# Expert layers as seven block products instead of eight, with the sums on VectorE and GpSimd

## The chip, the cores and the metric

The kernel runs on one core of one Trainium2 chip. The metric is the device time of one execution in microseconds. Three runs of the kernel before took 1371.4, 1369.11 and 1367.32 us; the median is 1369.11.

The profile names the engines so: PE is the TensorE matmul, PEld its weight loads, DVE is VectorE, ACT is ScalarE, POOL is GpSimd and SP is SyncE. SP, ACT and POOL also issue DMA transfers.

## What is computed

The whole program is a mixture of experts, a linear attention, a conditioned attention and two layers of local attention with a feed-forward network, over 4 x 512 tokens of width 256, all in float32. The change is in the mixture of experts alone:

```python
TOP_K = 2                                     # E = 8 experts, H = 256, M = 512
gate_w = jax.nn.softmax(gate, axis=-1)
topk_w, topk_i = jax.lax.top_k(gate_w, TOP_K)
cw = jnp.sum(jax.nn.one_hot(topk_i, E) * topk_w[..., None], axis=-2)
h1 = jax.nn.relu(jnp.einsum('bsh,ehm->bsem', x, W1) + b1)
h2 = jax.nn.relu(jnp.einsum('bsem,emn->bsen', h1, W2) + b2)
out_e = jnp.einsum('bsen,enh->bseh', h2, W3) + b3
return jnp.einsum('bseh,bse->bsh', out_e, cw)
```

Only the two experts chosen for a token matter, so the kernel sorts the 2 x 2048 pairs of token and expert by expert and computes only those.

## The kernel before

**Slots.** The sorted pairs are laid into slots of one expert each. `SLOTS` lists 24: 15 of 256 rows (two tiles of 128, `d.n == 2`) and nine of 128 rows. Their order is 1, 2, 2 twice, then 1, 2, 2, 2 three times, then 1, 2, 2, then 1, where 1 stands for a slot of 128 rows and 2 for one of 256; two more of 128 rows stand behind a branch and run only if they are needed. The 22 that always run are the list `often`. `rowtok` says which token each row of a slot takes, and `goal` to which row of the DRAM buffer `ys` its result goes. A row of padding has the entry 0 in both maps: it gathers token 0 and writes row 0 of `ys`.

**One slot.** `loads` brings the expert's weights in three transfers on SP: `w1` (with the biases of both layers in its first eight columns), `w2` and `w3`, two buffers each. A buffer's next load waits until everything that read the buffer's last contents is done. `gather` fetches the slot's rows of x with one indirect DMA per tile, issued by POOL, transposes them on PE, and copies them to SBUF as `xbT`. `layer` is used twice: h1 from `xbT` with `w1` (two chunks of the contraction), and h2 from h1 with `w2` (four chunks). In a slot of 256 rows a layer has four output blocks of 128 units, each a chain of 128x128 weights against 256 tokens, two blocks to a PSUM bank; `relu` adds the bias and takes the maximum with zero, alternately on ACT and DVE. `last` is the third layer: tokens as the stationary side, `w3` moving, then an addition of the bias on DVE into `ob`, and one indirect DMA per tile that scatters `ob` to `ys`, issued by POOL. A scatter waits until the scatter before it has landed, since both write `ys`.

**Order.** In the loop over `often` (from line 1506), iteration j writes down: layer one of slot j, `last` of slot j-1, loads and gather of slot j+1, one of the `later` weight loads, layer two of slot j. The framework's scheduler may move instructions within this, by priority and its own estimate of time, except those given to `keep_in_program_order`. PE's instructions are kept so only where `PE.in_order()` is set; in the loop that is the transposes of a gather.

**PSUM.** `banks("ps0", mm=4, tp=2, acc=2)` gives four banks to the layers, two to transposes and two to the third layer.

**Afterwards.** `results` reads `ys` back by token, and `weighted` makes the weighted sum into the four tiles `y[b]`, which stand unused until then.

Of the kernel before, what the change touches and what calls it, by code (L numbers as in the profile page):

```python
# [12 lines left out]
F32 = mybir.dt.float32  # L13
I32 = mybir.dt.int32
AF = mybir.ActivationFunctionType
# [5 lines left out]
NT = S // 128  # L21
# [21 lines left out]
NRARE = 2  # L43
NROWT = 2 * NPAIR + NHALF
NHI = 2 * NROWT
MCONST = (128, 128 + NE, 2 * NE, 2, NE * NE, NHI, 2 * B * NT, 64, NE)
NMC = sum(MCONST)


# [18 lines left out]
def adaln_attn_ffn_kernel(ctx: ExitStack, tc: tile.TileContext, a: dict, out: bass.AP):  # L68
# [1093 lines left out]
    with ExitStack() as abc:  # L1162
# [5 lines left out]


        with ExitStack() as moe:  # L1170
            moe.enter_context(banks("ps0", mm=4, tp=2, acc=2))
            xp = moe.enter_context(tc.tile_pool(name="xp", bufs=1, reuse_waits="tile"))
            ew = moe.enter_context(tc.tile_pool(name="ew", bufs=2, reuse_waits="tile"))
            hp = moe.enter_context(tc.tile_pool(name="hp", bufs=2, reuse_waits="tile"))
# [13 lines left out]
            for n in MCONST:  # L1188
                parts.append(mc[:, at : at + n])
                at += n  # L1190
            mtri, mtiles, mthr, mslot, mlow, miota, mtok, mfold, mwt = parts


            ys = dr.tile([1 + 2 * B * S, H], F32, tag="ys", name="ys")
            xall = a["x"].rearrange("b s h -> (b s) h")


# [201 lines left out]
            pmap2 = acct("pmap2")  # L1399
            for q in range(2):  # L1400
                PE.matmul(pmap2[64 * q : 64 * q + 64, :NROWT], mfold, half_map[:, :, q], start=True, stop=True)
            goal = xp.tile([128, NROWT], I32, tag="goal", name="goal")
            nc.vector.tensor_copy(goal, pmap2[:, :NROWT])
            rowtok = xp.tile([128, NROWT], I32, tag="rowtok", name="rowtok")
            nc.vector.tensor_scalar(rowtok, pmap2[:, :NROWT], -1.0, 0.0, ALU.add, ALU.max)
            nc.vector.tensor_single_scalar(rowtok, rowtok, B * S - 1, op=ALU.bitwise_and)


            def busy(n):
# [7 lines left out]

            def relu(dst, src, bias):
                if turn[0]:
                    nc.scalar.activation(dst, src, AF.Relu, bias=bias)  # L1420
                else:
                    nc.vector.tensor_scalar(dst, src, bias, 0.0, ALU.add, ALU.max)  # L1422


            def place(kind, i):
# [11 lines left out]
                d.w3 = ew.tile([128, 5, H], F32, tag="w3", name="w3")  # L1437
                nc.sync.dma_start(d.w3, we[:, 8 + 6 * ME :].rearrange("p (c m) -> p c m", m=H))

            def gather(j, d):  # L1440
                xb = hp.tile([128, 2, H], F32, tag="xb", name="xb", bufs=3)
                for i in range(d.n):
                    r = place(d.n, SLOTS[j][0]) + i
                    nc.gpsimd.indirect_dma_start(
                        out=xb[:, i, :], out_offset=None, in_=xall,
                        in_offset=bass.IndirectOffsetOnAxis(ap=rowtok[:, r : r + 1], axis=0))
                n = d.n * 128
                pt = tpt("pxb")
                with PE.in_order():
                    for c in range(2):  # L1450
                        for i in range(d.n):
                            PE.transpose(pt[:, c * n + i * 128 : c * n + (i + 1) * 128],
                                         xb[:, i, c * 128 : (c + 1) * 128], ident)
                xbT = hp.tile([128, 2, 256], F32, tag="xbT", name="xbT")
                evac(xbT[:, :, 0:n], pt[:, : 2 * n].rearrange("p (c t) -> p c t", t=n))
                d.xbT = xbT

            def layer(d, src, tag, w, bias):
                n = d.n * 128
# [14 lines left out]
                        relu(dst[:, m, 0:n], ps[:, i * n : (i + 1) * n], d.w1[:, bias + m : bias + m + 1])  # L1474
                return dst

            def last(j, d):
                ps = acct("po")
                for i in range(d.n):
                    mm(ps[:, i * H : (i + 1) * H],  # L1480
                       [(d.h2[:, c, i * 128 : (i + 1) * 128], d.w3[:, c, :]) for c in range(4)])
                ob = hp.tile([128, 2, H], F32, tag="ob", name="ob", bufs=3)
                nc.vector.tensor_tensor(
                    ob[:, 0 : d.n, :], ps[:, : d.n * H].rearrange("p (i h) -> p i h", h=H),
                    d.w3[:, 4, :].unsqueeze(1).to_broadcast([128, d.n, H]), ALU.add)
                for i in range(d.n):
                    r = place(d.n, SLOTS[j][0]) + i
                    nc.gpsimd.indirect_dma_start(
                        out=ys, out_offset=bass.IndirectOffsetOnAxis(ap=goal[:, r : r + 1], axis=0),
                        in_=ob[:, i, :], in_offset=None)  # L1490


            later = {
# [5 lines left out]
            cond_weights(wp, lambda name, load: later.update({name: load}))  # L1499
            cw_ = {}  # L1500

            ds = [SimpleNamespace() for _ in SLOTS]
            loads(0, ds[0])
            gather(0, ds[0])
            often, rare = ds[:-NRARE], range(len(ds) - NRARE, len(ds))
            for j, d in enumerate(often):
                if j == len(often) - 1:
                    aside = conditions(cw_, wp)
                    next(aside)
                if j == len(often) - 2:  # L1510
                    halves = nc.values_load(nhalf[0:1, 0:1], min_val=0, max_val=2 * NE)
                if j == 1:
                    weights()
                h1 = layer(d, d.xbT, "h1", d.w1[:, 8:].rearrange("p (c m) -> p c m", m=ME), 0)
                if j:
                    last(j - 1, ds[j - 1])
                if j + 1 < len(often):
                    loads(j + 1, ds[j + 1])
                    gather(j + 1, ds[j + 1])
                    if j > 1 and later:  # L1520
                        name, behind[0] = next(iter(later)), True
                        cw_[name] = later.pop(name)()
                        behind[0] = False
                d.h2 = layer(d, h1, "h2", d.w2, 4)
            last(len(often) - 1, often[-1])

            next(aside)
# [1 line left out]
            with tc.If(halves > NHALF - NRARE):  # L1529
                for j in rare:  # L1530
                    d = ds[j]
                    loads(j, d)
                    gather(j, d)
                    h1 = layer(d, d.xbT, "h1", d.w1[:, 8:].rearrange("p (c m) -> p c m", m=ME), 0)
                    d.h2 = layer(d, h1, "h2", d.w2, 4)
                    last(j, d)
# [213 lines left out]
def _shape_constants():  # L1750
    f = np.float32
    p = np.arange(128)
    bmask = np.repeat((p[:, None] // 32 == p[None, :] // 32).astype(f)[:, None, :], 4, axis=1)
    hmask = np.where(p[:, None] // CHD == np.arange(8)[None, :], CHD**-0.5, 0.0)
    hmask = np.concatenate([hmask, p[:, None] // CHD % 2 == np.arange(2)[None, :]], axis=1).astype(f)
    i, j = p[:, None], p[None, :]
    lmask = np.concatenate([np.where(j >= i, 0.0, MASKED), np.where(j <= i, 0.0, MASKED)], axis=1).astype(f)

    kmask = np.concatenate([(j >= i % 64)[:, :64], (j <= i % 64)[:, :64], j >= i], axis=1).astype(f)

    e = np.arange(NE)
    thr = np.concatenate([256 * e + 128, 256 * e])
    slot = np.full((128, 2), -1)
    slot[: len(SLOTS), 0] = [i if n == 2 else NPAIR + i // 2 for i, n in SLOTS]
    slot[: len(SLOTS), 1] = [-1 if n == 2 else i for i, n in SLOTS]
    tile, expert = p // NE, p % NE
    mconst = np.concatenate(
        [(p[:, None] < p[None, :]).astype(f),
         ((tile[:, None] < tile[None, :]) & (expert[:, None] == expert[None, :])).astype(f),
         (expert[:, None] == e[None, :]).astype(f), np.tile(thr, (128, 1)).astype(f), slot.astype(f),  # L1770
         np.tile((e[None, :] <= e[:, None]).reshape(-1), (128, 1)).astype(f), np.tile(np.arange(NHI), (128, 1)).astype(f),
         (np.arange(2 * B * NT)[None, :] * 128 + p[:, None] + 1).astype(f),
         (p[:, None] % 64 == np.arange(64)[None, :]).astype(f),
         np.tile(np.where(e == NE - 1, 1 - NE, 1), (128, 1)).astype(f)], axis=1)

    pos = np.arange(S, dtype=f)
    inv = f(10000.0) ** np.repeat(np.arange(0, H, 2, dtype=f) / f(H), 2)
    peT = np.ascontiguousarray(np.sin(pos[:, None] / inv[None, :]).astype(f).T)

    half = np.arange(0, DHD, 2, dtype=f)  # L1780
    freqs = pos[:, None] * (f(1.0) / f(10000.0) ** (half / f(DHD)))[None, :]
    base = (half + f(0.4 * DHD)) / f(1.4 * DHD)
    scale = base[None, :] ** ((pos - f(S // 2)) / f(WIN // 2))[:, None]
    cos, sin = np.cos(freqs).astype(f), np.sin(freqs).astype(f)
    parts = []
    for sc in (f(8.0) * scale, f(1.0) / scale):
        c, s = cos * sc, sin * sc
        parts += [np.concatenate([c, c], 1), np.concatenate([-s, s], 1)]
    rot = np.stack(parts).astype(f).reshape(4, NT, 128, DHD).transpose(2, 0, 1, 3)
    return {"mconst": mconst, "bmask": bmask, "hmask": hmask, "lmask": lmask, "kmask": kmask, "peT": peT, "rot": rot}  # L1790
# [81 lines left out]
```

## Time and profile before

| what | us |
|---|---|
| median of three runs | 1369.11 |
| the profiled execution | 1364.1 |
| its span, first to last instruction | 1362.3 |
| PE busy (span share 96%) | 1302.8 |
| DVE busy (47%) | 645.4 |
| ACT busy (41%) | 563.9 |
| POOL busy (17%) | 227.1 |
| expert stage, 42 to 315 us: PE busy in it | 270.7 |
| the same stage: DVE, ACT, POOL busy | 58.5, 43.5, 77.4 |

A line of the profile's groups reads: source line, engine, operation, tile written and tiles read, shape, count; then the busy time of the group, the mean duration of one in ns, and the idle time of that engine just before, with what ended it. `ph` is the PSUM bank of the first two layers, `po` that of the third, `pxb` that of the transposes. Matmuls overlap in the array, so one record is longer (379 ns for 256 columns) than the distance to the next. A float32 matmul has two MATMUL records and two weight loads. Lines of a timeline or a chain begin with the start in us from the span's start and the length of the merged piece. A line of windows gives, for each stretch, busy time and count of PE, PEld, DVE, ACT and POOL, then PE's clock, the share of DMA busy and GB/s. Sources and tiles give the minimum, median and maximum duration in ns.

### The profile page before, as it was taken

The numbers are of one execution on the slowest core, as the hardware profiler recorded it, in microseconds if no ns is written. First come the engines' busy times: TensorE is split into PE (matmuls) and PEld (weight loads), VectorE is DVE, ScalarE is ACT, GpSimd is POOL, SyncE is SP. The second block draws the span as 40 slices with busy tenths as digits, with TensorE's granted clock in tenths as the row PEclk, the third lists the DMA queues.
The fourth block names the chain that finished last, engine by engine and source line by source line (L and its number), as shares of the span: only waits on it lengthen the run. The fifth ranks groups of instructions, "written<-read, shape, count | busy, mean of one in ns | idle before, by whom it ended". The sixth has DMA issues, their size and how long they took to land.

```text
span 1362.3 us, 25766 instructions
## 1 busy us (share of the span) xinstructions
PE 1302.8 (96%) x10700; PEld 850.1 (62%) x10700; DVE 645.4 (47%) x1343; ACT 563.9 (41%) x1111; POOL 227.1 (17%) x223
## 2 busy tenths in 40 slices
PE   5899999998999999999999999999999998999998
PEld 4788888884666644444435665766555566667654
DVE  6222212125777743332226777764362767765421
ACT  4111111125555456565655646552223565463111
POOL 1324322211000020010103322100030312210010
PEclk7999999999999999999999999999999999999999
DMA  4577666644000000000201011211001011011000
GB/s 135 205 244 280 228 231 240 211 155 136 1 1 1 0 1 1 1 0 1 90 5 67 13 29 37 81 42 25 24 1 43 24 34 26 19 42 50 20 20 26
DMA packets 43110, 95.02 MB, mean 70 GB/s; under 512 B 9568, under 2 KB 25192, under 8 KB 40168
## 3 DMA queue, kind: packets, MB, share of 16 engines
q1 hardware_dynamic: 37560, 81.81, 18.1%
q0 software_dynamic: 3792, 10.24, 2.2%
q8 instruction: 88, 1.44, 0.4%
q10 hardware_dynamic: 1632, 1.21, 0.3%
q14 instruction: 38, 0.31, 0.1%
HBM read 83.95 MB, written 7.21 MB: 67 GB/s over the span
## 4 chain that ended last, share of the span: by engine, by line
PE 83%; DVE 7%; ACT 6%; issue 2%; DMA 1%; POOL 0%; POOLq 0%; SPq 0%; DVEq 0%; ACTq 0%
PE ph L82 14%; PE pdq L82 10%; PE sc L82 6%; PE pfy L82 6%; PE pug L82 5%; PE pua L82 5%; PE pv L82 5%; PE po L82 5%; PE pdy L82 4%; PE pn L82 3%; PE pz L82 2%; PE pds L82 2%; ACT p L685 2%; PE pqk L82 1%; PE pur L82 1%
## 5 line engine op out<-in xcount | busy, mean ns | idle before, releaser
L82 PE MATMUL pdq<-wqkv,yT 128*128 128x512 f32 x384 | 171.2, 596 | 6.0 <-ACT yT L613 4.1
L425 ACT ACTIVATE cex<-sc 128x512 f32<-128x512 f32 x256 | 131.8, 607 | 84.5 <-PE sc L82 84.4
L82 PE MATMUL ph<-h,w 128*128 128x256 f32 (+1 forms) x704 | 132.8, 346 | 1.6 <-DVE h L1422 1.6
L639 POOL TENSOR_TENSOR qr<-t,t 128x512 f32<-128x512 f32 x64 | 81.3, 1271 | 297.4 <-DVE t L636 282.8
L82 PEld LDWEIGHTS pdq<-wqkv,yT 128*128 128x128 f32 x384 | 71.4, 190 | 90.3 <-issue 76.9
L82 PEld LDWEIGHTS ph<-h,w 128*128 128x128 f32 x704 | 116.1, 191 | 13.7 <-DVE h L1422 1.9
L1420 ACT ACTIVATE h<-ph,w 128x256 f32<-128x256 f32 (+1 forms) x88 | 35.3, 437 | 190.9 <-PE ph L82 130.5
L1422 DVE TENSOR_SCALAR h<-ph,w 128x256 f32<-128x256 f32 (+1 forms) x88 | 36.1, 438 | 161.1 <-PE ph L82 102.6
L685 ACT ACTIVATE p<-pds,ss 128x192 f32<-128x192 f32 (+1 forms) x256 | 82.3, 434 | 12.5 <-PE pds L82 11.2
L82 PE MATMUL sc<-qm,kT 32*128 32x512 f32 x512 | 86.8, 639 | 0.0
L629 ACT ACTIVATE sq<-pdq 128x512 f32<-128x512 f32 x64 | 38.4, 601 | 97.1 <-POOL qr L639 50.2
L82 PE MATMUL pug<-hT,w 128*128 128x512 f32 x160 | 75.9, 597 | 0.0
L82 PE MATMUL pua<-hT,w 128*128 128x512 f32 x160 | 75.2, 592 | 0.0
L82 PE MATMUL ph<-xbT,w 128*128 128x256 f32 (+1 forms) x352 | 68.7, 347 | 0.5 <-ACT xbT L127 0.5
L82 PE MATMUL po<-w,h 128*128 128x256 f32 x296 | 67.6, 379 | 0.0
L395 POOL TENSOR_SCALAR fterm<-vw,faT 128x256 f32<-128x256 f32 x16 | 14.6, 922 | 312.1 <-DVE cr L385 259.6
L789 ACT ACTIVATE gl<-pug,cols 128x512 f32<-128x512 f32 x40 | 27.3, 687 | 86.5 <-PE pug L82 86.4
L82 PEld LDWEIGHTS ph<-xbT,w 128*128 128x128 f32 x352 | 58.5, 191 | 7.2 <-ACT xbT L127 0.7
L82 PE MATMUL pfy<-w,uA 128*128 128x256 f32 x256 | 61.2, 382 | 0.0
L82 PEld LDWEIGHTS pn<-p,v 64*64 64x64 f32 x1792 | 44.1, 136 | 27.4 <-issue 10.1
L82 PE MATMUL pv<-cex,v 128*32 128x512 f32 x512 | 61.2, 597 | 0.0
L82 PEld LDWEIGHTS po<-w,h 128*128 128x128 f32 x296 | 55.7, 190 | 8.1 <-ACT h L1420 0.9
(304 smaller groups left out, 2182.7 us busy)
## 6 DMA issues: line engine op xcount, KB each, us to landing
w<-in_moe_w_dram SPq DMA_DIRECT2D x22, 1024.0 KB
w<-in_moe_w_dram SPq DMA_DIRECT2D x22, 640.0 KB
w<-in_moe_w_dram SPq DMA_DIRECT2D x22, 516.0 KB
zb<-rows SPq DMA_DIRECT2D x32, 256.0 KB
g<-ys SPq DMA_DIRECT2D x6, 512.0 KB
wqkv<-in_f_wqkv_dram SPq DMA_DIRECT2D x2, 1536.0 KB
w<-in_f_w_dram SPq DMA_DIRECT2D x2, 1408.0 KB
out_dram<-yc SPq DMA_DIRECT2D x16, 128.0 KB
```

What stands on the lines that cost most here:

```text
L82: cls._queue(nc.tensor.matmul(*args, **kw))
L395: nc.gpsimd.tensor_scalar_mul(fterm[:, t, :], vw, W["faT"][:, t, b : b + 1])
L425: nc.scalar.activation(ex[:, i, :], pss[2 * j + i], AF.Exp, scale=CHD**-0.5)
L629: nc.scalar.activation(sq, p3, AF.Square)
L639: nc.gpsimd.tensor_tensor(qr_t[:, s], t1, t2, ALU.add)
L685: nc.scalar.activation(p[:, at : at + n], pss[j // 2][r][:, at % 384 : at % 384 + n], AF.Exp, scale=d.ss[:, j, 1, 2 * c + r : 2 * c + r + 1])
L789: nc.scalar.activation(gl, pg, AF.Gelu, bias=col("bg", l * (NU + 1) + i))
L1420: nc.scalar.activation(dst, src, AF.Relu, bias=bias)
L1422: nc.vector.tensor_scalar(dst, src, bias, 0.0, ALU.add, ALU.max)
```

## The change

A layer of a 256-row slot is seen as a product of 2x2 blocks: the weights halved along inputs and along outputs, the tokens halved along inputs and into two tiles of 128. Eight block products make it plainly. The change computes it with seven, from sums and differences of blocks, for the 14 slots of 256 rows other than the first (`few`). Four sums of weight blocks for each layer (`weight_sums`) are made on POOL; four of token blocks (`token_sums`) on DVE; each product gets a PSUM bank of its own, and DVE adds products together (`plus`) before ACT takes bias and relu.

```diff
-            moe.enter_context(banks("ps0", mm=4, tp=2, acc=2))
+            moe.enter_context(banks("ps0", mm=5, tp=1, acc=2))
...
+            def weight_sums(s, w):
+                n = w.shape[1] // 2
+                a11, a12, a21, a22 = (w[:, j0 * n : (j0 + 1) * n, 256 * i0 : 256 * i0 + 256]
+                                      for i0 in range(2) for j0 in range(2))
+                pinned(nc.gpsimd.tensor_tensor(s[0], a21, a22, ALU.add))
+                pinned(nc.gpsimd.tensor_tensor(s[1], s[0], a11, ALU.subtract))
+                pinned(nc.gpsimd.tensor_tensor(s[2], a11, a21, ALU.subtract))
+                pinned(nc.gpsimd.tensor_tensor(s[3], a12, s[1], ALU.subtract))
...
+                b11, b12, b21, b22 = blocks(src)
+                _, c12, c21, c22 = blocks(src if psum is None else psum)
...
+                pinned(nc.vector.tensor_tensor(t[:, 0], c12, b11, ALU.subtract))
+                pinned(nc.vector.tensor_tensor(t[:, 1], c22, t[:, 0], ALU.subtract))
+                pinned(nc.vector.tensor_tensor(t[:, 2], c22, b12, ALU.subtract))
+                pinned(nc.vector.tensor_tensor(t[:, 3], c21, t[:, 1], ALU.subtract))
+                return t
...
+                def block(i0, j0, out, p, other):
+                    plus(out, p, other)
+                    for m in range(2):
+                        pinned(nc.scalar.activation(
+                            dst[:, 2 * i0 + m, 128 * j0 : 128 * j0 + 128], out[:, m], AF.Relu,
+                            bias=d.w1[:, bias + 2 * i0 + m : bias + 2 * i0 + m + 1]))
...
+                p1 = product(whole(0, 0), src[:, 0:n, 0:128])
+                pinned(nc.scalar.copy(e1, p1))
+                p2 = product(whole(0, 1), src[:, n : 2 * n, 0:128])
+                block(0, 0, e15, p2, e1)
+                p4 = product(whole(1, 1), t[:, 3])
+                p6 = product(summed(1), t[:, 1])
+                plus(e16, p6, e1)
+                p5 = product(summed(0), t[:, 0])
+                plus(e15, p5, e16)
+                p7 = product(summed(2), t[:, 2])
+                plus(e17, p7, e16)
+                block(1, 0, e1, p4, e17)
+                block(1, 1, e16, p5, e17)
+                p3 = product(summed(3), src[:, n : 2 * n, 128:256])
+                block(0, 1, e15, p3, e15)
```

`product` makes two chains of 128x128 weights against 128 tokens, one for each half of 256 output units: two matmuls in layer one, four in layer two. The products with plain weights (p1, p2, p4) come first. The weight sums and the token sums of h1 lie in the tiles `y[b]`. The token sums of `xbT` take one operand of each from the bank of the transposes in PSUM; those of h1 take both from SBUF.

The loop gets an order of its own, all of PE's instructions in it kept, and those of the other engines that `pinned` marks (sums, additions, relus, gathers, scatters, `ob`):

```diff
+                with PE.in_order():
+                    if d.few:
+                        h1 = layer_few(d, d.xbT, d.t1, "h1", w1, d.s1, 0)
+                        t2 = token_sums(h1)
+                    else:
+                        h1 = layer(d, d.xbT, "h1", w1, 0)
+                    if j + 1 < len(often):
+                        loads(j + 1, after)
...
+                    if after.few:
+                        first_sums(after)
+                    if j + 2 < len(often):
+                        fetch(j + 2, ds[j + 2])
+                    if j:
+                        last(j - 1, ds[j - 1])
+                    if j + 1 < len(often):
+                        turn_tokens(after)
+                    d.h2 = layer_few(d, h1, t2, "h2", d.w2, d.s2, 4) if d.few else layer(d, h1, "h2", d.w2, 4)
+                if after.few:
+                    second_sums(after)
```

`gather` is cut in two: `fetch`, the indirect DMAs, now two slots ahead, and `turn_tokens`, the transposes and the copy to `xbT`, always on ACT. Last, rows of padding no longer all write row 0: `ys` has 128 rows more, and padding in partition p writes row 1 + 2·B·S + p.

```diff
+            goalf = xp.tile([128, NROWT], F32, tag="goalf", name="goalf")
+            nc.vector.scalar_tensor_tensor(goalf, pmap2[:, :NROWT], 0.0, maside.to_broadcast([128, NROWT]),
+                                           ALU.is_equal, ALU.mult)
+            goal = xp.tile([128, NROWT], I32, tag="goal", name="goal")
+            nc.vector.tensor_tensor(goal, pmap2[:, :NROWT], goalf, ALU.add)
```

## The prediction

> **What bounds the kernel now.** I read the page first, then the chain of waits, the timelines of PE and POOL and the windows of the expert stage (42 to 315 us). The busy rows by slices of 34 us:
>
> ```profile
> PE   5899999998999999999999999999999998999998
> POOL 1324322211000020010103322100030312210010
> ```
>
> PE is full through the stage and POOL a quarter busy. The chain of waits there, by start and length, is PE alone. One 256-row slot:
>
> ```profile
> 92.31 10.36 PE ph L82 x48
> 102.68 3.45 PE po L82 x16
> 106.13 0.22 PE pxb L86 x2
> ```
>
> Each float32 product is two MATMUL records. 48 records with 256 columns take 10.36 us (0.216 each), the third layer 3.45, a pair's four transposes 0.44 (0.11 each): 14.25 us per slot. So every microsecond off PE counts here, and so does every stall. PE timeline, a run of each width, and two windows (a 256-row slot, and a piece around a 128-row one):
>
> ```profile
> 92.15 7.07 PE L82 MATMUL ph<-h,w 128*128 128x256 f32 x32
> 118.77 3.74 PE L82 MATMUL ph<-h,w 128*128 128x128 f32 x32
> ...
> 99.06:113.10 14.04, 14.04 (x68) 12.33 (x67) 3.32 (x7) 1.21 (x3) 5.32 (x6) 1.00 0.64 225
> 113.10:122.35 9.25, 9.25 (x70) 8.79 (x69) 1.99 (x4) 1.57 (x4) 2.50 (x3) 1.00 0.72 251
> ```
>
> 32 records of 128 columns run every (3.74-0.275)/31 = 0.112 us; weight loads (8.79 of 9.25 us busy) don't hold them below that. DVE and ACT have room (3.3 and 1.2 of 14 us). POOL's timeline and its two relevant groups:
>
> ```profile
> 107.89 0.95 POOL L1444 DMA_INDIRECT xb<-in_x_dram,rowtok  x1 [0.30 <-issue]
> 109.14 1.00 POOL L1488 DMA_INDIRECT ys<-ob,goal  x1 [0.30 <-issue]
> 112.64 0.98 POOL L1488 DMA_INDIRECT ys<-ob,goal  x1 [2.50 <-DMA ys<-ob,goal]
> ...
> L639 POOL TENSOR_TENSOR qr<-t,t 128x512 f32<-128x512 f32 x64 | 81.3, 1271 | 297.4 <-DVE t L636 282.8 <-PE pdy L82 13.5 <-PE pds L82 1.0
> L396 POOL TENSOR_TENSOR fterm<-fterm,crows 128x256 f32<-128x256 f32 x16 | 11.3, 725 | 0.0
> ```
>
> An indirect DMA costs POOL 0.97 + 0.30 us, and a slot's second scatter stands 2.5 us until the first has landed. Last, DVE beside POOL, from two sources and the two timelines at 1145 us:
>
> ```profile
> L1558 DVE SCALAR_TENSOR_TENSOR ymoe<-g,m,g x16: 472/478/2222, 321.5 to 339.2; 128x256 f32<-128x256 f32 x16
> L825 DVE TENSOR_TENSOR yc<-pfy,yc x32: 369/415/425, 932.7 to 1357.2; 128x256 f32<-128x256 f32 x32
> ...
> 1145.47 5.08 DVE L732 TENSOR_TENSOR oT<-oT,zb 128x512 f32<-128x512 f32 x2
> ...
> 1144.85 2.40 POOL L775 TENSOR_TENSOR yc<-yc,drows 128x1024 f32<-128x1024 f32 x1 [3.38 <-DVE hn L762]
> 1147.33 2.67 POOL L778 TENSOR_TENSOR yc<-yc,xres 128x1024 f32<-128x1024 f32 x1
> ```
>
> A DVE operation with both inputs in SBUF (0.478) took 2.222 when a POOL addition ran (322.44, 2.34 us): it ended 0.28 after POOL did. Two such in a row (0.69 each, alone) took 5.08 beside two POOL additions: each waited for one, they take turns. L825, with one input in PSUM, never exceeded 0.425.
>
> **What the Trainium skill says.** "SBUF — State Buffer", Who interferes with whom: a Vector operation with two SBUF inputs and a GpSimd operation that reads SBUF block each other, the later for the whole of the earlier; one SBUF input doesn't. The lines above agree. "GPSIMD Engine Reference", 3.1: about 2.6 cycles per element for a two-input add, which makes 1.1 us of 512 elements; measured 1.271, which I use. "TensorE: Matmul & The Clock Gate", LDWEIGHTS: columns / 1.2 ns, 107 for 128; records 0.112 apart agree with a floor near it. "DMA: Bandwidth & Descriptors", Two DMAs through the same engine are not ordered: the later must wait for the earlier's semaphore; that is the 2.50 us.
>
> **What PE gains.** Fourteen slots are `few`. Before: 24 products, 48 x 0.216 = 10.4 us. After: layer one 7 products of 2 matmuls, layer two 7 of 4, 42 x 2 x 0.112 = 9.4. Gain 0.96 a slot, 13.4 us in all, if PE never waits. Seven block products save an eighth, and half of it goes to the narrower records. Slots are then 13.3 us (3.14 layer one, 3.45, 0.44, 6.27 layer two).
>
> **What POOL gains in work.** 4 x 0.725 + 4 x 1.271 = 8.0 us a slot, in one pinned queue with gathers and scatters. A group of one 128-row and three 256-row slots takes POOL 3 x 8.0 + 14 x 1.27 + 3 x 2.5 + about 6 delays of 0.28 by DVE = 51 us. PE needed 3 x 14.25 + 7.3 = 50.1 before, and 47.2 after. A group with two takes POOL 34.9 against 35.8 before. So POOL alone eats the gain, even with no idle.
>
> **What DVE and ACT gain.** ACT's 16 activations of 128 columns, from SBUF, have no row; PSUM ones took 0.367 (128) and overlap by some 0.04: I take 0.33 to 0.35 each, bounds 0.28 and 0.40. ACT then has 7 us a slot, DVE about 10 (14 additions at 0.42, four token sums at 0.42, four at 0.28, `ob` 0.69): not bounds by sum, but they lie in a chain. A slot inherits layer two's last relus, which end 2.2 us into it, so the copy of p1 ends at 2.6; p7 wants p1's bank back at 2.2 and waits 0.4 us. The chain of sums and three pairs of relus from there has h1 whole at 7.1 us (after a 128-row slot 5.9, as ACT is free). The four sums of h1, 0.36 apart, end at 8.7. Layer two's third product wants the last of them: it is due at 3.5 + 3.45 + 0.44 + two products of 0.9 = 9.3. Alone it just fits; with a POOL addition in each gap it doesn't.
>
> **Where POOL stands then.** Scatters, gathers and sums go in this order in iteration j: first sums (j+1), gathers (j+2), scatters (j-1), second sums (j+1). First sums need w1, whose load is issued when layer two's last relu has let go of the biases (2.4 us into the slot) and lands some 3.5 us later (before: issue 100.26, and the rate row sums to its 516 KB by about 103). For a group H, P1, P2, P3, in each slot's time:
> H (9.3 us long with the pair's third layer): first sums of P1 5.9 to 8.8, gathers to 11.4, scatters with their landing to 16.3, second sums of P1 to 21.4, that is 7.0 to 12.1 of P1.
> P1: token sums are through at 7.4, in time, but p6 wants the second of the weight sums, at 9.9, when it could start at 8.3: stall 1.9 with the rest. P1 is 13.5 long.
> P2: first sums done at 1.8, just in time; two gathers, one scatter; second sums (its own) 5.7 to 10.8. The token sums at 7.1 take turns with three of them: 8.6, 10.2, 11.8, 12.1. Stall 2.9, with the bank 3.3.
> P3: second sums from 4.0; token sums end at 10.4 against 9.0: 1.4, with the bank 1.8.
> The next H finds POOL free at 2.0, ready for 5.9: it repeats. A group of two stalls 1.9 + 2.2 (one gather less). Slot 2, behind plain slots, I put at 1.5, as the least of them. Three groups of three, two of two: 3 x 7.0 + 2 x 4.1 + 1.5 = 30.7 us. Less 13.4: 17.3 us slower.
>
> **The rest costs nothing.** `goal` gets one DVE operation behind `rowtok`, off the gather's path (0.2 us nearer, within noise); the rows of padding get targets of their own, which might shorten a landing (bounds: 0 and 1 us of the 2.5, POOL's only). Weights keep their SP order; behind their waits stand only the `later` loads. The pinned order removes the scheduler's freedom, but its places for third layer and transposes are those of the chain above. Late gathers (P2's are issued until 2 us into P1) end inside the stalls counted.
>
> **Rivals.**
> 1. POOL keeps ahead (landings of 1 us, sums early in the slot). Then only the banks (0.4) and a little are lost: 13.4 less 3 to 5, about 9 us faster, 1360. For: POOL had 75% to spare on average. Against: its sum above. 28%.
> 2. Queues give way and POOL's rate alone decides: three groups at +0.9, two at -0.9, slot 2 at -1: about 1369, no change. 12%.
> 3. The forecast, slower by a collision of token sums with weight sums in layer two, decisive from 0.96 us a slot; worked out as 2.2 us. 47%, its own range 1374 to 1398.
> 4. All four sums collide from the first: 4 x 1.55 from 7.1 is 13.3 against 9.3, 4 us a slot, 56 less 13.4: 1412. For: POOL works through layer two in every slot. Against: part of the sums are through by then. 13%.
>
> **Numbers.** The sum is against 1364.1 us (span 1362.3 plus 1.8 around it), giving 1381. The median of three runs, 1369.1, lies 5.0 above that execution, so I forecast 1369.1 + 17.3 = 1386. The range, 1357 to 1404, takes in rivals 1 and 2 and leaves out most of 4. A kernel like this is measured to about 0.3%, 4 us. Faster: rival 1 but for its low end, and a tail of 2 and 3, 0.32; same 0.10; slower 0.58.
>
> **What would show it.** PE records of ph 128 wide, 0.112 apart, 1176 of them in the `few` slots: right on gain. DVE's h1 sums (SBUF, 128x256) with a mean well above 0.42, and PE's idle before ph released by them or by POOL's sums, 2 us a slot: right on loss. POOL near 90% busy or waiting from 60 to 290 us. If PE stays gapless there, or the h1 sums stay at 0.42, I am wrong, and rival 1 holds.

## The result, and the profile after

Four runs of the changed kernel took 1410.05 to 1417.02 us, median 1412.28; four of the kernel before, beside them, 1368.84. The ratio is 1.032, with an interval of 1.0289 to 1.0351: slower by 43 us, where 17 were forecast. The profiled execution took 1412.23 us, its span 1410.2.

The busy rows of its page, by slices of 35 us:

```profile
PE   5988789798999999999999989999999998999998
POOL 1455866745000010101102312200011213210110
```

In the stage (slices 2 to 10) PE has lost its nines, and POOL has doubled. The last matmul of the stage's third layers starts at 354.5 us instead of 313.4: 41.1 us of the loss lie in the stage. The two profiled executions are 47.9 us apart; the other 6.8 us lie behind the stage and were not followed up (executions of one kernel spread by 4 to 7 us). The windows of the stage give, as before: length, busy time and count of PE, PEld, DVE, ACT, POOL, PE's clock, DMA share, GB/s. The two short ones cover a stall of PE and what follows it:

```profile
42.00:315.00 273.00, 238.65 (x1705) 224.46 (x1705) 125.64 (x322) 92.15 (x274) 168.51 (x168) 0.96 0.59 200
...
93.00:97.40 4.40, 1.04 (x9) 0.85 (x8) 1.30 (x6) 0.69 (x2) 3.64 (x4) 0.94 0.71 220
97.40:100.30 2.90, 2.90 (x14) 2.90 (x15) 0.42 (x1) 0.00 (x0) 2.90 (x3) 0.50 0.07 28
```

PE was busy for 270.7 of these 273 us before; now for 238.7, at a clock of 0.96 instead of 1.00. POOL is busy for 168.5 us instead of 77.4, so it isn't full: much of the rest it stands waiting. PE's gaps of over 0.25 us between 50 and 345 us add up to 36.5 us (3.6 before). The view of waits (engine, tile and line, what it waited for, us in total, times, longest) between 42 and 360 us says for what:

```profile
POOL ys L1581 <- DMA ys<-ob,goal: 68.8, 15, 8.4
...
PE ph L82 <- POOL ymoe L1501: 22.3, 7, 5.6
...
PE pxb L86 <- DMA xb<-in_x_dram,rowtok: 9.1, 5, 3.3
...
PE ph L82 <- DVE ymoe L1521: 4.8, 5, 1.9
```

So PE mostly waits for the second of four weight sums (L1501), then for gathered rows, and only then for the token sums of h1 (L1521). POOL itself waits 68.8 us for scatters to land. Both timelines, from a 128-row slot into the 256-row slot behind it, and again a group later:

```profile
85.36 0.96 POOL L1447 DMA_INDIRECT xb<-in_x_dram,rowtok  x1 [0.30 <-issue]
86.62 1.00 POOL L1581 DMA_INDIRECT ys<-ob,goal  x1 [0.30 <-issue]
93.66 0.99 POOL L1581 DMA_INDIRECT ys<-ob,goal  x1 [6.03 <-DMA ys<-ob,goal]
94.67 1.27 POOL L1500 TENSOR_TENSOR ymoe<-w 128x512 f32<-128x512 f32 x1
96.02 1.26 POOL L1501 TENSOR_TENSOR ymoe<-ymoe,w 128x512 f32<-128x512 f32 x1
...
141.28 4.68 POOL L1692 TENSOR_TENSOR xres<-xres,crows 128x1024 f32<-128x1024 f32 x2
145.90 0.74 POOL L1500 TENSOR_TENSOR ymoe<-w 128x256 f32<-128x256 f32 x1
146.58 2.36 POOL L1692 TENSOR_TENSOR xres<-xres,crows 128x1024 f32<-128x1024 f32 x1
148.87 0.74 POOL L1501 TENSOR_TENSOR ymoe<-ymoe,w 128x256 f32<-128x256 f32 x1
```

```profile
90.28 1.95 PE L82 MATMUL ph<-h,w 128*128 128x128 f32 x16
92.81 1.16 PE L82 MATMUL ph<-ymoe,w 128*128 128x128 f32 x8 [0.58 <-DVE ymoe L1521]
97.33 4.36 PE L82 MATMUL ph<-ymoe,ymoe 128*128 128x128 f32 x24 [3.36 <-POOL ymoe L1501]
...
149.67 2.93 PE L82 MATMUL ph<-t,ymoe 128*128 128x128 f32 x12 [5.57 <-POOL ymoe L1501]
```

The two scatters stand in front of the second sums in POOL's pinned queue. The first is issued at 86.62, the second goes out at 93.66 only, 6.03 us after POOL was ready for it. In the five such places the wait is 6.03, 6.18, 6.48, 8.37 and 6.31 us. In the trace's packets the 128 KB of this first scatter move at 91.0 to 92.7 us, among the last of the loads of `w1` (516 KB) and `w2` (1 MB), which SP had issued at 86.12 and 86.84 and which move at 87.0 to 93.2. The sums follow, and PE's product p6 (`ph<-ymoe,ymoe`) starts 0.05 us after the second sum has ended (96.02 + 1.26). At 141 us something stands in the queue that no one had put there: three of four additions to the residual (L1692, 2.35 us each), work for a later stage that isn't pinned. In the kernel before they ran at 127.6 us, in POOL's idle time; now the scheduler laid them between two weight sums, and PE stood still for 5.57 us.

The four token sums of h1, from the groups by shape (busy time, mean in ns, idle before):

```profile
L1518 DVE TENSOR_TENSOR ymoe<-h 128x256 f32<-128x256 f32 x14 | 10.2, 730 | 17.7 <-ACT h L1546 17.7
L1519 DVE TENSOR_TENSOR ymoe<-h,ymoe 128x256 f32<-128x256 f32 x14 | 7.9, 561 | 0.5
L1521 DVE TENSOR_TENSOR ymoe<-h,ymoe 128x256 f32<-128x256 f32 x14 | 6.9, 493 | 0.0
L1520 DVE TENSOR_TENSOR ymoe<-h 128x256 f32<-128x256 f32 x14 | 6.9, 492 | 0.0
```

Together 2.28 us a slot instead of 4 x 0.42: the turn-taking with POOL is there, as the Trainium skill says ("SBUF — State Buffer", Who interferes with whom), but it costs 0.6 us a slot. Of the 56 sums 45 took 0.42 us as if alone; eleven took 0.94 to 1.55.

For the following it helps to have one yardstick: the interval between the starts of two third layers. From that of a 128-row slot to that of the 256-row slot behind it lies layer two of that slot and layer one of the next. Before, this interval was 12.53 us in all five groups where both slots now have seven products; after, it was 18.40, 24.70, 19.54, 21.20 and 19.07. These five intervals alone grew by 40.3 us. In the others the saved matmuls and further stalls (one of 14.25 us became 17.39) nearly cancel.

### The profile page after: what moved, and what is told of

It is laid out like the page before. It is cut to its first block, busy times and chain, and to the rows that moved or that the text cites. A ratio compares the mean times of both kernels' runs of the same rounds, so it can differ in the third digit from the quotient of the medians.

```text
span 1410.2 us, 27427 instructions
## 1 busy us (share of the span) xinstructions
PE 1311.5 (93%) x11204; PEld 869.9 (62%) x11204; DVE 732.0 (52%) x1585; ACT 627.1 (44%) x1318; POOL 339.1 (24%) x335
## 4 chain that ended last, share of the span: by engine, by line
PE 60%; DVE 6%; ACT 5%; issue 2%; DMA 2%; POOL 0%; SPq 0%; ACTq 0%; POOLq 0%; DVEq 0%
PE pdq L82 9%; PE sc L82 6%; PE pfy L82 6%; PE pug L82 5%; PE pua L82 5%; PE pv L82 5%; PE pdy L82 4%; PE pn L82 3%; PE pds L82 2%; PE pz L82 2%; ACT p L685 1%; PE pqk L82 1%; PE pck L82 1%; PE pf L82 1%; PE pur L82 1%
## 5 line engine op out<-in xcount | busy, mean ns | idle before, releaser
L1546 ACT ACTIVATE h<-e,w 128x128 f32<-128x128 f32 x224 | 71.6, 390 | 128.6 <-DVE e L1551 125.7
L1551 DVE TENSOR_TENSOR e<-ph,e 128x256 f32<-128x256 f32 x196 | 76.0, 420 | 86.9 <-PE ph L82 69.2
L395 POOL TENSOR_SCALAR fterm<-vw,faT 128x256 f32<-128x256 f32 x16 | 14.6, 924 | 312.2 <-DVE cr L385 259.7
L82 PE MATMUL ph<-ymoe,ymoe 128*128 128x128 f32 x336 | 47.7, 307 | 16.8 <-POOL ymoe L1501 16.8
L82 PE MATMUL ph<-h,w 128*128 128x128 f32 (+1 forms) x480 | 62.5, 287 | 0.4 <-ACT h L1423 0.4
L82 PE MATMUL pn<-p,v 64*64 64x128 f32 (+1 forms) x1792 | 50.3, 252 | 11.4 <-DVE p L688 10.5
L82 PEld LDWEIGHTS ph<-h,w 128*128 128x128 f32 x480 | 59.2, 195 | 1.7 <-ACT h L1423 0.6
L630 DVE TENSOR_REDUCE ss<-sq 128x8 f32<-128x512 f32 x64 | 43.5, 679 | 32.0 <-ACT sq L629 32.0
```

The lines of the kernel that those rows point to most:

```text
L82: cls._queue(nc.tensor.matmul(*args, **kw))
L395: nc.gpsimd.tensor_scalar_mul(fterm[:, t, :], vw, W["faT"][:, t, b : b + 1])
L630: nc.vector.reduce_sum(ss[:, t, s, :], sq, axis=AX.X)
L1546: pinned(nc.scalar.activation(dst[:, 2 * i0 + m, 128 * j0 : 128 * j0 + 128], out[:, m], AF.Relu, bias=d.w1[:, bias + 2 * i0 + m : bias + 2 ...
L1551: pinned(nc.vector.tensor_tensor(out, p, other, ALU.add))
```

## The experiments

Two theories stood at the start. **Queue**: POOL's queue in a 128-row slot makes the second weight sums late. **Collision**, that of the forecast: token sums of h1 that take turns with POOL. Ratios are against the kernel before.

### The new order with eight products

```diff
-            ds = [SimpleNamespace(few=n == 2 and j > 1) for j, (_, n) in enumerate(SLOTS)]
+            ds = [SimpleNamespace(few=False) for _ in SLOTS]
```

> The changed kernel with no slot few: new order, five and one PSUM banks, gathers two slots ahead and the new targets of padding stay, every layer is the plain one. Queue theory (the loss is POOL's queue with the weight sums in it): about as the kernel before, 1364 to 1373 us, PE without gaps over 0.5 us. Rival, that the fixed order itself or the late gathers lose the time: 1390 or more.

`order_only` took 1366.79 us, ratio 1.000 (0.9985 to 1.0015). Intervals of 12.53, 12.37, 10.92 and 14.25 us, as before. Taken together, the written order, the gather two slots ahead, the division of the banks and the rows for padding cost or bring nothing beyond 0.15%.

### Weight sums left out

```diff
...
-                pinned(nc.gpsimd.tensor_tensor(s[0], a21, a22, ALU.add))
-                pinned(nc.gpsimd.tensor_tensor(s[1], s[0], a11, ALU.subtract))
-                pinned(nc.gpsimd.tensor_tensor(s[2], a11, a21, ALU.subtract))
-                pinned(nc.gpsimd.tensor_tensor(s[3], a12, s[1], ALU.subtract))
+                s[:] = [a21, a11, a22, a12]
```

> The weight sums are left out: the products take plain blocks of the weights where sums stood, so POOL adds nothing and the output is another. PE, DVE and ACT do the same work. Queue theory and collision theory both: the stalls go, 1354 to 1364 us, PE's gain of 13 us minus banks. Rival, that chains of DVE and ACT or the 128-wide records hold PE: above 1380.

`no_weight_sums`, whose products take plain blocks where sums stood, took 1358.77 us, ratio 0.9937 (0.9917 to 0.9956). The weight sums on POOL carry the whole loss: 53 us, and 9 of gain without them. This alone doesn't say how: it takes the queue's work and the collisions away together. The intervals show the gain: 10.92 became 10.59 (layer one, 0.33), 12.37 became 11.71 (layer two, 0.66). But 12.53 became only 12.43, where both parts should have made it 11.54: behind a 128-row slot, whose own third layer is short, the sums of h1 come some 0.5 us late; the rest is mostly the wait for p1's bank in layer one.

### Sums of h1 left out

```diff
+                if n == 2:
+                    return [b12, b22, b21, b12]
                 pinned(nc.vector.tensor_tensor(t[:, 0], c12, b11, ALU.subtract))
...
```

> The four token sums of h1 are left out, the products take plain blocks of h1 in their place; the output is another. POOL's work and queue stay. Queue theory: little changes, 1402 to 1412 us, the long intervals behind 128-row slots stay at 18 to 24 us. Collision theory (the prediction's): 1375 to 1385, as no operation with two SBUF inputs is left on DVE in these slots.

`no_h1_sums` took 1410.18 us, ratio 1.0308 (1.0278 to 1.0338): nothing is won. The view of waits, of this kernel:

```profile
PE ph L82 <- POOL ymoe L1501: 28.2, 8, 5.0
```

With the h1 sums gone, PE waits longer for the weight sums (28.2 us against 22.3). The collision theory falls, for the change as it stands.

### Second sums in front of the scatters

In iterations of slots with eight products, the second sums move from behind the scatters to the place behind the gathers; nothing else.

```diff
                     if j + 2 < len(often):
                         fetch(j + 2, ds[j + 2])
+                    if after.few and not d.few:
+                        second_sums(after)
                     if j:
                         last(j - 1, ds[j - 1])
...
-                if after.few:
+                if after.few and d.few:
                     second_sums(after)
```

> In the iterations of slots that are not few, the second weight sums of the next slot stand on POOL ahead of the two scatters instead of behind them. Queue theory: the wait for a landing no longer delays these sums, the intervals behind 128-row slots fall from 18 to 24 us to 13 to 15, in all 20 to 30 us faster than the changed kernel: 1380 to 1392. Collision theory: the same number of operations meet, no change beyond 5 us.

`sums_first` took 1391.05 us, ratio 1.0177 (1.0129 to 1.0224): a move of four instructions takes back 21 us. POOL's timeline, in the place shown above:

```profile
86.70 1.28 POOL L1500 TENSOR_TENSOR ymoe<-w 128x512 f32<-128x512 f32 x1
...
90.52 1.53 POOL L1503 TENSOR_TENSOR ymoe<-w,ymoe 128x512 f32<-128x512 f32 x1
92.21 1.00 POOL L1581 DMA_INDIRECT ys<-ob,goal  x1 [0.15 <-issue]
94.89 0.98 POOL L1581 DMA_INDIRECT ys<-ob,goal  x1 [1.68 <-DMA ys<-ob,goal]
```

The sums are through at 92.1 instead of 99.7, and POOL stands 1.68 us instead of 6.03 for the landing of the scatter, which it now issues when the packets of `w1` and `w2` have all but moved (the last ends at 93.2). The five intervals are 13.5, 20.5, 13.6, 13.6 and 13.6; the 20.5 is the place with the residual additions.

### Scatters apart

The second scatter of a pair waits for the head of the next iteration, by when the first has landed.

```diff
...
+                if j > 1 and ds[j - 2].n == 2:
+                    scatter(j - 2, ds[j - 2], 1)
                 with PE.in_order():
...
-                for i in range(d.n):
-                    r = place(d.n, SLOTS[j][0]) + i
+                scatter(j, d, 0)
```

> The second scatter of a pair is moved to the head of the next iteration, ahead of the first sums; every operation is kept. Queue theory, with the landing of the first scatter as the decisive term: POOL's idle time before scatters falls from 69 us to under 15, the intervals behind 128-row slots to 13 to 16 us, the kernel to 1374 to 1388 us. Rival, that POOL's amount of work and not its waits decides: above 1400.

`spread` took 1389.37 us, ratio 1.0149 (1.011 to 1.0189). POOL's wait for landings falls from 68.8 to 29.9 us, and as much is won as with the sums in front: either way out of the landing wait does. The forecast of 1374 to 1388 us, with a wait under 15 and intervals of 13 to 16, was missed (the five are 14.6, 19.5, 17.3, 14.5 and 15.0; the 19.5 is again the place with the residual additions).

### Residual additions kept behind the stage

`sums_first`, and with it:

```diff
-                nc.gpsimd.tensor_tensor(
-                    xres[b], xres[b], row("bo").unsqueeze(1).to_broadcast([128, NT, H]), ALU.add)
+                tc.keep_in_program_order(nc.gpsimd.tensor_tensor(
+                    xres[b], xres[b], row("bo").unsqueeze(1).to_broadcast([128, NT, H]), ALU.add))
```

> sums_first, and POOL's four residual additions of 2.4 us (xres plus its bias row, of the stage behind) kept in program order, so that none of them comes between the weight sums. If they cost what the gap of slot 7 shows: 5 to 8 us below sums_first, 1383 to 1386 us. If they only fill time that POOL would wait: no change.

`first_and_after` took 1388.14 us, ratio 1.0147 (1.0123 to 1.0172), 3 us less than `sums_first`, which is within the noise of the two. In the profiled executions the interval of 20.5 is 13.5 now, and the stage's last third-layer matmul starts 6.6 us earlier (323.7 instead of 330.3); but 3.6 us are given back behind the stage. There the four additions now run in one row of 9.8 us, and in the 60 us behind the stage PE is idle for 7.5 us instead of 4.4.

### All three moves

> All three moves together, 14 slots few: scatters apart, second sums first behind slots that are not few, residual additions behind the stage. Queue theory: 1362 to 1374 us, with what is left lost to the token sums' collisions and late gathers. Rival, that POOL's sum of work bounds: 1376 or more.

`spread_first_after` took 1385.65 us, ratio 1.0118 (1.0092 to 1.0145), on the rival's side of the line. The first two moves are worth 21 and 23 us alone, the third 3 on top of the first; together they make 27. The waits of this kernel:

```profile
POOL ymoe L1500 <- DMA w<-in_moe_w_dram: 28.6, 5, 11.3
...
PE pxb L86 <- DMA xb<-in_x_dram,rowtok: 11.0, 9, 2.5
...
PE ph L82 <- DVE ymoe L1521: 2.7, 4, 1.2
```

PE's MATMULs wait for no weight sum any more. What is late are the gathers, which stand in the same queue behind the sums: in the three 256-row slots of a group POOL works almost without a pause (133.76 to 161.2 us), and the interval from the first of these slots to the second is 15.1 to 17.4 us, where it is 13.55 without weight sums. In the 128-row slot, though, POOL stands still, for landings and until `w1` has been loaded:

```profile
167.00 0.97 POOL L1584 DMA_INDIRECT ys<-ob,goal  x1 [2.27 <-DMA ys<-ob,goal]
172.27 0.72 POOL L1500 TENSOR_TENSOR ymoe<-w 128x256 f32<-128x256 f32 x1 [4.29 <-DMA w<-in_moe_w_dram]
```

Over the stage POOL is busy for 182.6 of 282.3 us. Not all that is left lies in the stage: of the 23.9 us between this profiled execution and that of the kernel before, 10.9 do, and 13.0 behind it.

### What is left: the collision, the place or the sum of POOL's work?

Four kernels. `three_no_h1` is `spread_first_after` without the sums of h1. `dve_three` is `spread_first_after` with the first sums on DVE:

```diff
...
-                weight_sums(d.s1, d.w1[:, 8:].rearrange("p (c m) -> p c m", m=ME))
+                weight_sums(d.s1, d.w1[:, 8:].rearrange("p (c m) -> p c m", m=ME), nc.vector)
...
```

`dve_first_after` makes the same edit in `first_and_after`. `first_spaced` is `sums_first` with three residual additions pinned one each to 128-row slots.

> spread_first_after (1385.65) with the token sums of h1 left out, so that layer two of the 14 slots takes blocks of h1 instead of their sums: part of the computation is left out. With the queue put right, do the sums of h1 that take turns with POOL hold PE now? Collision theory: the third 256-row slots in a row, whose intervals are 15 to 17.4 us against 13.5, fall to 13.5: about 10 to 13 us, 1373 to 1376. Theory that POOL's work and the gathers bound: the intervals stay, 1382 to 1386.

> All 14 slots with seven products, the second sums ahead of the scatters behind a 128-row slot (sums_first), and the residual additions one each in three 128-row slots. There POOL has second sums, gathers and scatters of its own. If the sum of POOL's work bounds these groups (51 us against PE's 47), three additions of 2.4 us cost what they cost in the other places: 1386 to 1391, no better than sums_first (1391) by more than 5. If only the place between the sums was bad: 1380 to 1384.

> spread_first_after (1385.65) with the first sums (four of 128x256 a slot) on VectorE instead of GpSimd. It takes 14 x 2.9 us from POOL, which then has 42 us of work in a group of one and three against PE's 47. If POOL's summed work is what is left, the late gathers go, and most of the remaining 26 us over the ideal (1359) go: 1362 to 1374. If the order of the queue is what is left, or VectorE's part of the chain gets late instead (it waits for w1 in front of its additions), 1382 or more.

> first_and_after (1388.14) with the first sums on VectorE: scatters in pairs as in the change. POOL stands 6 us behind a first scatter in a 128-row slot, which with its 42 us of work makes 48 to 55 a group. If the landing still decides with less work, 1375 to 1386; if work alone was the matter, as dve_three, 1362 to 1374.

`three_no_h1` took 1391.47 us, ratio 1.0148 (1.0113 to 1.0184), more than either theory had named: nothing is won without the collisions here either. `first_spaced` took 1390.53, ratio 1.0169 (1.0137 to 1.0201): in the three places tried, these groups leave POOL no room for the additions. `dve_three` took 1371.79, ratio 1.0033 (1.0019 to 1.0046), and `dve_first_after` 1374.00, ratio 1.0039 (1.0023 to 1.0054): against the kernel before, measured beside them, some 13 us less each, by taking 2.9 us of work a slot from POOL and giving DVE 1.7. So what the moves left was in the main POOL's work in front of the gathers. Whether its amount decides or its place is not separated: the first sums stand ahead of the gathers, so the edit takes work away and lets the gathers go earlier at once, and gathers ahead of the first sums, all on POOL, were not tried. POOL's busy time alone, 65% of the stage in `spread_first_after`, doesn't bound it. With less of this work, scatters in pairs and scatters apart are 2.2 us from each other, within their intervals. In `dve_three` the waits are now:

```profile
PE ph L82 <- DVE ymoe L1521: 6.8, 10, 1.9
...
PE pxb L86 <- DMA xb<-in_x_dram,rowtok: 1.1, 1, 1.1
```

Now, with POOL in time, the sums of h1 are what PE waits for most. They are not the remaining loss of 0.3%: in the profiled execution (1366.87 us, the fastest of 15) the last third-layer matmul starts at 312.4 us, 1.0 before that of the kernel before. Behind the stage, where the four residual additions are, PE is idle for 8.0 us in 60, instead of 4.3; that is of the size of the loss, which was not taken apart further.

### Fewer slots with seven products

Only the nine slots behind another 256-row slot: POOL then has one slot's time without sums in each group, and the third layer in front of layer two is one of 256 rows (3.45 us instead of half of it), so that PE wants the second weight sum later.

```diff
-            ds = [SimpleNamespace(few=n == 2 and j > 1) for j, (_, n) in enumerate(SLOTS)]
+            ds = [SimpleNamespace(few=j > 1 and n == 2 == SLOTS[j - 1][1]) for j, (_, n) in enumerate(SLOTS)]
```

> Only slots of 256 rows behind another of 256 rows are few: nine instead of fourteen, the five behind 128-row slots are plain. Queue theory: POOL has 40 us less to add and the place where it was late is gone; PE gains 0.65 a slot and loses a little to collisions: 1360 to 1370 us, no worse than before. Rival, that any weight sums on POOL stall PE: 1380 or more.

`few_behind_pair` took 1369.16 us, ratio 1.0008 (0.9992 to 1.0023). One interval of 19.73 us is left, with the residual additions between the sums again. Two kernels put these elsewhere:

> Seven products only in the nine slots that stand behind another 256-row slot, and the four residual additions of POOL kept in program order, that is behind the expert stage. With few_behind_pair alone one slot of nine had an interval of 19.7 us, since three residual additions stood between its weight sums. If those additions are the cause, that interval falls to about 13.6 and the expert stage ends some 6 us earlier (307 instead of 313 us); from 1369 this gives 1363, if the additions cost nothing behind the stage, and up to 1367, if they are in the way there (some 2 to 4 us were given back in first_and_after). If POOL's pace is the cause in any place, the time stays at 1369.

> As few_pair_after, but three of the residual additions stand, one each, in iterations of 128-row slots whose next slot has plain weights, where POOL has nothing else to do, and the fourth in front of the stage. The slot with 19.7 us should fall to about 13.6 and nothing is given back behind the stage: 1361 to 1364, that is 0.3 to 0.5% faster than before. If POOL's pace in those iterations already decides, an addition of 2.4 us pushes gathers back and the time stays at 1366 or more.

Kept behind the stage (`few_pair_after`): 1368.09 us, ratio 0.9994 (0.998 to 1.0009). The stage is 6.3 us shorter than in `few_behind_pair`, as expected, but the time is hardly less. In the profiled executions 4.5 us are given back behind the stage: the four additions run there in one row of 9.8 us from 317.5, and PE's waits for DVE in that place are 5.6 us instead of 2.4. Spaced out in 128-row slots (`few_pair_spaced`): 1364.58, ratio 0.9977 (0.9965 to 0.9989), a little faster than before; one interval of 17.3 us is left. That one goes, too, with the first sums on DVE:

> few_pair_spaced (1364.58) with the first sums on VectorE. If POOL's lateness is what still holds its third slots (intervals 13.9 to 17.3 against 13.5), about 5 us go: 1358 to 1362. If VectorE gets late instead: 1364 or more.

`dve_pair` took 1357.37 us, ratio 0.9922 (0.9909 to 0.9936): 0.8% faster than the kernel before, about as much as the kernel without weight sums (0.6%). PE's row of its page and its window of the stage:

```profile
PE   5999999999999999999999899999999988999998
```

```profile
42.00:315.00 273.00, 271.29 (x1794) 245.86 (x1794) 131.73 (x328) 89.23 (x247) 126.43 (x115) 1.00 0.65 223
```

PE is full again (271.3 of 273 us, clock 1.00), with POOL busy for 126 us instead of 168.5. Removing the landing wait itself, with a second buffer for `ys`, was not tried.

## Why the prediction was wrong in size and cause, and right in direction

**Right.** The direction, but in part by luck. Of the 30.7 us of stalls in the forecast, 5 x 1.9 = 9.5 stood where the loss arose, in P1's wait for weight sums; less the gain of 13.4 they alone would have made the kernel 4 us faster. What made the forecast slower was the other 21.2 us, nearly all the collision and the banks. That rival 4 names 1412, where 1412.28 was measured, is luck too: its mechanism is the collision as well. What held: the records are 128 wide and 0.112 us apart, and the gain of 0.96 us a slot shows in the intervals (0.33 and 0.66). Of the 13.4 us in all, 10.0 arrive in the stage where no weight sum is made (the last third-layer matmul of `no_weight_sums` starts at 303.4 us for 313.4). This is rival 1, "13.4 less 3 to 5, about 9 us faster": 8.9 in the medians. The order, `goal` and the padding rows cost nothing, taken together (`order_only`). The weight sums took 0.73 to 0.76 and 1.27 to 1.30 us, near their price. One remark of the text was off: of the eighth saved, 1.30 us of 10.37, the narrower records take back 0.34, a quarter and not half; the sum itself used the right 0.96.

**The step that failed** is POOL's clock in H: "scatters with their landing to 16.3, second sums of P1 to 21.4", and from it "stall 1.9 with the rest". The first sums started at 81.0 in the trace, for 5.9 in the text; on that clock the gathers end at 11.2 (predicted 11.4), the scatters at 19.6 (16.3) and the second sums at 24.6 (21.4). Nearly the whole error is the landing: 2.5 us taken from one line of the timeline, 6.03 in this place and up to 8.37 in the others. The view of waits of the kernel before shows that the one line was no safe price:

```profile
POOL ys L1488 <- DMA ys<-ob,goal: 53.9, 16, 8.1
```

A mean of 3.4 and a longest of 8.1 us: the 2.5 was neither a mean nor a bound. Its timeline gives the same five places, the pair scattered in a 128-row slot, as 4.29, 5.15, 4.21, 3.48 and 3.85 us; the 2.50 was taken from a 256-row slot. Why these waits grew once more, to 6.03 and above, stays open. In the kernel before POOL had time for them; they decide where sums are queued behind.

Set against `no_weight_sums`, where these intervals are 12.4 us, the five P1 intervals hold 40.8 us of stall, where 9.5 were forecast, and all others 10.3, where 21.2 were forecast. Together 51.1, less the 10.0 of gain, make the 41.1 us of the stage.

**Also mis-sized: the collision.** "Stall 2.9" in P2 and "1.4" in P3 came from token sums that take turns with three weight sums each. Measured, the turns cost 0.6 us a slot, and leaving the token sums out brought 2 of 43 us, which is within the noise. With POOL so late, these sums seldom met: 11 of 56 took over 0.5 us. With the queue put right (`spread_first_after`) 22 of 56 did, at 1.2 us a slot, yet there too leaving them out won nothing (`three_no_h1`). So the collision is refuted as the cause, in the change and with the three moves made. The sign that the forecast had named for it, PE's idle time released by token sums "or by POOL's sums, 2 us a slot", came true at 1.9 us a slot (27.1 in all), but it could not tell the two causes apart: 22.3 of the 27.1 are waits for weight sums.

**Not foreseen.** First, that the scheduler would put work that isn't pinned between pinned sums: at 141 us it made one interval 24.70. Second, the clock. The stage has eight windows of half clock of 3.41 us each, where the kernel before had none from 35 to 325 us. From 42 us to the last third-layer matmul PE is idle for 38.6 us (2.3 before), and 25.0 us of its busy time lie in half clock, which cost at most 12.5 us. These 36.3 and 12.5, less the 10.2 us that PE's busy time falls by in `no_weight_sums`, make 39 of the 41 us. Third, that gathers would get late: PE waits 9.1 us for them, where "end inside the stalls counted" had been written.

## What to carry to other kernels

Before work is put into a queue that holds waits, take the duration of these waits from their whole distribution and from the place where they will stand (here: the 128-row slots, beside the weight loads), and not from one line of the timeline; then put what the bottleneck engine waits for in front of them. When an order is pinned by hand, look for what isn't pinned on the same engine: here the scheduler laid three additions between two weight sums, and all four in one row behind the stage cost time there. And when an auxiliary engine pays for a saving on the bottleneck, compare its work and its waits per group with the bottleneck's time, before the saving is counted: the forecast itself had 51 us of POOL against 47 of PE. What won was moving a third of the sums' time to another engine, giving up five of the slots and spacing the additions out.

## What the hardware showed unexpectedly

**Landings beside weight loads.** For a scatter of 128 KB that POOL issued at 86.62, between SP's loads of 516 KB and 1 MB, POOL stood until 93.7 us; when it was issued at 92.21 (`sums_first`) POOL went on after 2.7 us. In the first case the scatter's packets began to move at 91.0 us, when most of the loads had passed. That the loads are the cause was not tried by itself: gathers of POOL's own were under way, too, in the first case until 89.4 us.

**The clock falls after less than a whole idle window.** The half-clock spells begin on a grid of 3.413 us, the window that the Trainium skill gives ("TensorE: Matmul & The Clock Gate", What's actually happening). But its advice of "No PE-idle gaps >~3µs between matmul bursts" (Why this matters for your kernels) is too mild here: between 42 and 345 us, in the traces of both kernels and of all fifteen experiments, every window at full clock with 1.97 us or more of PE idle time in it was followed by one at half clock, and none with 1.79 us or less; between, both occurred. (Idle is what no PE record covers, and the ends of these are modelled.) In the changed kernel a gap of 1.89 us at 217.5 was enough, while one of 2.59 us at 136.3 lay across two windows and cost no clock. Behind 345 us some windows with less idle time were followed by half clock, too (one of 0.83 us in `sums_first`), so this is not the whole rule.
